# Image 0's queries and keys in a two-level form, and layer 1's value-output product ahead of them

## The chip, the cores and the metric

One core of a Trainium2 chip runs the whole kernel. Its engines are TensorE (PE in the profile, its weight loads PEld), VectorE (DVE), ScalarE (ACT), GpSimd (POOL) and SyncE (SP), whose queue issues nearly all DMAs here. The metric is the device time of one execution in microseconds; shown is the median of several runs.

## The reference

Two attention blocks, one after the other, on 8 images of 512 channels and 1024 positions, all in float32. Layer 0 has 8 heads of 64 channels; layer 1 has one head of 512.

```python
# layer 0
h = group_norm(x, gn_weight, gn_bias)              # 32 groups
qkv = einsum('oc,bct->bot', w_qkv, h) + b_qkv      # 8 heads: q, k, v of 64 channels
weight = softmax(einsum('bct,bcs->bts', q * scale, k * scale))
a = einsum('bts,bcs->bct', weight, v)
x = x + einsum('oc,bct->bot', w_proj, a) + b_proj
# layer 1
xn = group_norm(x, gamma, beta)                    # 8 groups
q, k, v = conv1x1(xn, q_w, q_b), conv1x1(xn, k_w, k_b), conv1x1(xn, v_w, v_b)
out = softmax(q^T k / sqrt(512)) v
x = x + conv1x1(out, p_w, p_b)
```

## The kernel before

**Products with fewer multiplications.** A convolution is a product of a 512x512 weight matrix with a 512x1024 image. The kernel makes it by the Strassen-Winograd scheme: both matrices are cut into 2x2 blocks, seven sums of blocks of each ("factors", 1 to 7) are multiplied pairwise, and sums of the seven products give the result. `wino` (L229) does this once: seven products, each of four matrix multiplications of 128x128 weights with 512 columns, so 28. `by_channel`, `by_token`, `biased` and `conv` are built on it. `conv2` (L536) with `inner_steps` (L452) does it twice: each of the seven products is again cut in halves, so there are 49 products of 128x128 weights with 256 columns. For that it needs the image's factors of factors (`inner_factors`, L423: seven times four subtractions of 128x256) and the weights' second sums (`keep2_steps`, L302: four operations of 128x896 on a weight tile, the results stored in DRAM by seven DMAs of 448 KB). `load_weight` brings them back from DRAM in the order of the list `uses`.

**Steps.** Within a convolution the products are taken in the order 1, 6, 2, 5, 7, then 3 and 4. The last two wait in the list `tail` and run after step 1 of what follows; `finish()` empties the list at once. In `inner_steps` step 1 fills a PSUM bank of pool "a", ScalarE copies it to a bank of pool "b" (L482), and step 6 adds onto this copy. `conv2` takes its seven outer products in the pairs (1, 5), (2, 6), (3, 4) and the single (7), the last two interleaved. `hooks` are functions that run behind each of these four parts, `background` a list from which each step takes one or more.

**The start** (`prologue`, L936). It loads the raw weights of layer 1, transposes keys and queries with `natural` (L893), multiplies them (`product`, "m": layer 1's scores need only this product of the two), normalizes image 0, and makes its values (`by_token`), queries and keys (`conv`, one level) with weights whose first sums `prepare` (L281) has made. Between these, the second sums of v are made on VectorE, those of q, k, m and p on GpSimd, for the later images. After the keys come the transposes of layer 1's value weights (wv), the bias rows (`bias_products`, L919) and the product "z" of layer 1's value and output weights. Then `attention0` of image 0 begins; z's own sums are made during it.

**Order.** A scheduler orders the instructions of each engine ahead of time; `tc.keep_in_program_order` pins one behind the one traced before it on its engine, and all TensorE work is pinned. Each engine, and each DMA queue, then works strictly in this order.

**Memory.** `big` is a pool of `NBIG` = 34 tiles of 4 KB a partition: images, factors, q, k, v, exponents and the results of sums on VectorE. `wpool` has 3 tiles for weights (14 KB a partition each). A tile's slot comes free when its last reader is done. PSUM has the pools "a", "b", "c" with two banks each, and "acc" with two.

Of the kernel before, what the change touches and what calls it, by code (L numbers as in the profile page):

```python
# [9 lines left out]
F32 = mybir.dt.float32  # L10
I32 = mybir.dt.int32
AF = mybir.ActivationFunctionType
# [3 lines left out]
P = 128  # L16
EPS = 1e-5
ORDER = (1, 5, 2, 6, 7, 3, 4)
NBIG = 34

# [9 lines left out]
def two_attention_blocks_kernel(  # L30
# [143 lines left out]
    def main_path(ctx):  # L174
# [46 lines left out]


        tail = []

# [76 lines left out]

        def keep2_steps(n, t, engine=nc.gpsimd, pin=lambda ins: ins):  # L302

            if engine is nc.gpsimd:
                u = wpool.tile([P, 4, 7, P], F32, tag="w", name=f"prepare2_{n}")
                u = [u[:, i, :, :] for i in range(4)]
            else:
                u = [big_tile(f"prepare2_{n}_{i}", (P, 7, P)) for i in range(4)]
            quarter = lambda k, i: t[:, :, k, ts(i, P)]
            a11, a21, a12, a22 = quarter(0, 0), quarter(0, 1), quarter(1, 0), quarter(1, 1)  # L310
            s1, s2, s3, s4 = u
            def store():
                for j, f in enumerate((a11, a12, s4, a22, s1, s2, s3)):
                    pin(nc.sync.dma_start(wdram2[n][:, :, j, :], f))

            return [
                *(
                    lambda dst=dst, x=x, y=y, op=op: tc.keep_in_program_order(engine.tensor_tensor(dst, x, y, op))
                    for dst, x, y, op in (
                        (s1, a21, a22, ALU.add), (s2, s1, a11, ALU.subtract), (s3, a11, a21, ALU.subtract),  # L320
                        (s4, a12, s2, ALU.subtract),
                    )
                ),
                store,
            ]

        def keep2(n, t, engine=nc.gpsimd):
            for f in keep2_steps(n, t, engine):
                f()
# [72 lines left out]

        def biased(out, bias):
            def done(i, r, c, ps, u):
                oc = 2 * r + i
                dst = out[oc][:, ts(c, HT)]
                if u is None:
                    nc.scalar.activation(dst, ps, AF.Identity, bias=bias[:, oc : oc + 1])
                else:
                    nc.vector.scalar_tensor_tensor(dst, ps, bias[:, oc : oc + 1], u, ALU.add, ALU.add)  # L410

            return done

        def channel_tiles(name):
            return [big_tile(f"{name}_{c}") for c in range(KC)]

        def conv(wf, hf, bias, name, **kw):
            out = channel_tiles(name)
            by_channel(wf, hf, name, biased(out, bias), **kw)
            return out  # L420


# [112 lines left out]

        def conv2(n, f, bias, name, hooks=(), after=(), by_tokens=False, alone=False):  # L536

# [42 lines left out]
            def pair(s, products, y, x, final, **kw):  # L580
# [5 lines left out]

                w = weights2[s // 2][:, (0, 2, 0, 1)[s] :]

                def mm(ps, j, start):
                    for i, p in enumerate(products):  # L590
                        wt = w[:, i, j - 1, :]
                        if not by_tokens:
                            matmul(ps[:, i, :], wt, f[p][j], start=start and i == 0, stop=True, skip_group_check=True)
                            continue
                        for h in range(2):
                            matmul(
                                ps[:, i, ts(h, P)], f[p][j][:, ts(h, P)], wt,
                                start=start and (i, h) == (0, 0), stop=True, skip_group_check=True,
                            )
# [13 lines left out]
            second = []  # L613
            weights2 = [weight_part((n, 0))]
            pair(0, (1, 5), [(1, 0), (1, 1)], None, [])[1]()
            pair(
                1, (2, 6), [(0, 0), (0, 1)], [(1, 0), (1, 0)], [load_weight, lambda: biased_half(0, 0)], defer=second,
            )[1]()
            weights2.append(weight_part((n, 1)))
            ahead, end = pair(  # L620
                3, (3, 4), [(0, 1), (1, 0)], [(0, 1), (1, 0)], [load_weight, *after],
                order=(-3, 6, 5, -4, 7, 2) if alone else (-3, 6, -4, 2, 5, 7),
# [296 lines left out]
        def bias_products(lhs):  # L919

            n = len(lhs)
            ps = acc_tile("ps_bias")
            for kc in range(KC):
# [12 lines left out]
        def prologue():  # L936
            ident.append(big_tile("ident", (P, P)))
            make_identity(nc, ident[0])
            raw_k = raw("k", 5)
            raw_q = raw("q", 4)  # L940
            h0 = [load_x(0, c, "h0") for c in range(KC)]
            first = {n: prepare(n) for n in "vqk"}
            wk = natural(raw_k, "k", ("a", "b"))
# [13 lines left out]
            )  # L957
            raw_v = raw("v", 6)
            raw_p = raw("p", 7)
            for f in first["v"][1]:  # L960
                f()
            background.extend(steps)
            background.extend(first["q"][1])
            v = by_token(weight_factors(first["v"][0]), hf, "v0_0", middle=(2, 5, 6, 7), back=4)
            finish()
            run_background(len(background))
            keep2("v", first["v"][0], nc.vector)
            background.extend(first["k"][1])
            x1 = [load_x(1, c, "x1") for c in range(KC)] if B > 1 else []
            norm1 = GroupNorm(0, "0_1")  # L970
            background.extend(lambda c=c: norm1.stats(c, x1[c]) for c in range(len(x1)))
            q = conv(weight_factors(first["q"][0]), hf, pcols("bq0"), "q0_0")
            keep2("q", first["q"][0])
            keep2("k", first["k"][0])
            t, steps = prepare("m")
            k = conv(weight_factors(first["k"][0]), hf, pcols("bk0"), "k0_0", hooks=[[], [], [], [], steps])
            finish()
            p0, p0_steps = prepare("p")
            raw_p0 = raw("p0", 3)
            keep2("m", t)  # L980
            wv = natural(raw_v, "v", "bc")
            norm1.group_mean(acc_tile("gmean_0_1")[:, :KC])
            for f in p0_steps:
                f()
            keep2("p", p0)
            keep("p", p0)
            bias = bias_products([(wk, "bq1"), (raw_p, "bv1"), (raw_p0, "bv0")])
            product(wv, raw_p, "z", bank="b")
            norm1.affine(acc_tile("gvar_0_1")[:, :KC])
            t, steps = prepare("z")  # L990
            load = lambda: load_weight(tc.keep_in_program_order)
            second = keep2_steps("z", t, pin=tc.keep_in_program_order)
            later = {
# [14 lines left out]
        def load_again(b, c, what):  # L1008
            t = big_tile(f"{what}_{b}_{c}")
            nc.sync.dma_start(t, spills[b][c])  # L1010
            return t

        def all_background():
            run_background(len(background))

# [456 lines left out]
```

## Time and profile before

| What | Value |
|---|---|
| Median of 3 runs | 2768.27 us (2767.59 to 2768.7) |
| The profiled execution | 2768.3 us |
| Its span, first to last instruction | 2765.8 us |
| Mean granted TensorE clock | 0.999 |
| Busy in 49.7 to 97.8 us (48.1 us): TensorE, VectorE, ScalarE, GpSimd | 48.10, 32.58, 5.09, 18.01 us |
| Busy in 97.8 to 117.9 us (20.1 us): the same | 19.58, 11.38, 2.90, 16.49 us |
| DMA in these two stretches | 0.82 and 0.63 of the 16 engines |

The first of these stretches holds image 0's queries and keys, the second the transposes of wv, the bias rows and z. In the lines of the profile `psa_q` is a bank of pool "a" in the queries' convolution, `ps_wz` one of the product z, `sc` a bank of scores, `av` one of values by attention. An fp32 multiplication shows as two entries. A line in the timeline gives start, length, engine, line of the kernel, operation, the tile written and those read, the count, and in brackets the idle time before it and what ended it.

### The profile page before, as it was taken

Reading aid. Unit: us, or ns where it says so; the run is one execution under the profiler, and the core shown is the slowest. Engines: PE = TensorE matmul, PEld = TensorE weight load, DVE = VectorE, ACT = ScalarE, POOL = GpSimd, SP = SyncE. Lnnn points to the kernel's source line nnn. Section 1 sums busy time; section 2 is a strip of 40 time slices with the busy share of each in tenths; the row PEclk is TensorE's granted clock in tenths of the full one; section 3 lists DMA queues with packets and bytes.
Section 4 is the critical chain, followed back from the end, with each engine's and each line's share of the span. In section 5 each row is a group of like instructions: output and inputs, shape, how many; then the busy total and the mean of one; then the engine's idle time right before and its main releaser. Section 6 shows DMA issues by size and latency. Waiting matters only on the chain.

```text
span 2765.8 us, 36809 instructions
## 1 busy us (share of the span) xinstructions
PE 2753.6 (100%) x13436; PEld 1762.1 (64%) x13436; DVE 2045.6 (74%) x3214; ACT 998.4 (36%) x1307; POOL 1291.4 (47%) x1384
## 2 busy tenths in 40 slices
PE   9999999999999999999999999999999999999999
PEld 5437736776376853868538694486844968348585
DVE  6587777777777777777777867777678776787776
ACT  1253454214632146312453125531255313633130
POOL 2313605745067440774307752176621766146763
PEclk9999999999999999999999999999999999999999
DMA  7827412344113441144401443114521145112302
GB/s 265 253 91 252 181 32 70 138 159 166 40 63 138 170 162 32 63 161 167 150 24 63 177 182 119 32 55 184 196 98 49 58 153 216 59 54 97 142 24 74
DMA packets 126070, 332.60 MB, mean 120 GB/s; under 512 B 19831, under 2 KB 64695, under 8 KB 114362
## 3 DMA queue, kind: packets, MB, share of 16 engines
q1 hardware_dynamic: 125294, 329.75, 33.6%
q8 instruction: 108, 1.77, 0.3%
q14 instruction: 80, 0.66, 0.1%
q10 hardware_dynamic: 588, 0.42, 0.1%
HBM read 258.14 MB, written 71.99 MB: 119 GB/s over the span
## 4 chain that ended last, share of the span: by engine, by line
PE 99%; DVE 1%; DMA 0%; issue 0%; SPq 0%; DVEq 0%
PE sc L60 16%; PE av L60 16%; PE psb_av L60 6%; PE psb L60 5%; PE psa_av L60 4%; PE psc_av L60 4%; PE psc L60 4%; PE psa L60 3%; PE psb_v L60 3%; PE psb_k L60 3%; PE psb_p L60 3%; PE psb_q L60 3%; PE psb_g L60 3%; PE psb_z L60 3%; PE psc_z L60 2%; PE psa_k L60 2%
## 5 line engine op out<-in xcount | busy, mean ns | idle before, releaser
L700 DVE TENSOR_TENSOR sum<-sum,e 128x1024 f32<-128x1024 f32 x384 | 473.9, 1234 | 35.5 <-ACT e L696 0.9
L696 ACT ACTIVATE e<-sc 128x1024 f32<-128x1024 f32 x512 | 476.1, 1053 | 63.1 <-PE sc L60 62.6
L60 PE MATMUL sc<-q,k 64*128 64x512 f32 x2048 | 456.8, 596 | 0.0
L60 PE MATMUL av<-e,v 128*64 128x512 f32 x2048 | 453.4, 595 | 0.0
L60 PEld LDWEIGHTS sc<-q,k 64*128 64x128 f32 x2048 | 190.1, 185 | 245.9 <-ACT e L696 120.9
L60 PEld LDWEIGHTS av<-e,v 128*64 128x64 f32 x2048 | 141.4, 137 | 299.0 <-issue 288.2
L434 POOL TENSOR_TENSOR inner_h<-x 128x256 f32<-128x256 f32 x16 | 14.8, 924 | 415.9 <-DVE x L1028 415.9
L698 DVE TENSOR_TENSOR sum<-e,e 128x1024 f32<-128x1024 f32 x64 | 79.9, 1249 | 103.6 <-ACT e L696 103.6
L719 ACT COPY a<-av 128x512 f32<-128x512 f32 x64 | 37.5, 586 | 320.1 <-PE av L60 280.6
L126 POOL TENSOR_TENSOR rstd<-ve,mhalf 128x4 f32<-128x4 f32 x16 | 18.8, 1177 | 274.0 <-DVE ve L124 274.0
L60 PE MATMUL psb<-inner,inner_h 128*128 128x256 f32 x448 | 115.6, 380 | 0.0
L60 PE MATMUL psa_av<-e,z 128*128 128x512 f32 x256 | 112.5, 592 | 0.0
L482 ACT COPY psb_v<-psa_v 128x512 f32<-128x512 f32 (+1 forms) x28 | 14.5, 517 | 232.5 <-DVE x L845 176.6
L60 PEld LDWEIGHTS psb<-inner,inner_h 128*128 128x128 f32 x448 | 84.5, 190 | 13.6 <-POOL inner L449 2.1
L60 PE MATMUL psb_z<-w_z,inner_h 128*128 128x128 f32 x672 | 87.5, 276 | 0.0
L60 PE MATMUL psb_g<-inner_h,w_m 128*128 128x256 f32 x336 | 84.9, 381 | 0.0
L776 ACT ACTIVATE e<-e 128x1024 f32<-128x1024 f32 x64 | 65.1, 1052 | 46.7 <-DVE e L766 25.6
L60 PEld LDWEIGHTS psb_z<-w_z,inner_h 128*128 128x128 f32 x672 | 81.4, 192 | 0.5
L60 PEld LDWEIGHTS psa_av<-e,z 128*128 128x128 f32 x256 | 47.4, 190 | 53.6 <-issue 51.7
L771 POOL TENSOR_TENSOR e<-e,e 128x512 f32<-128x512 f32 x64 | 79.3, 1271 | 2.0 <-DVE e L766 1.8
L571 POOL TENSOR_TENSOR v<-v,v 128x256 f32<-128x256 f32 x28 | 20.1, 726 | 125.3 <-DVE u_v L566 121.3
L820 POOL TENSOR_TENSOR t<-e,t 128x1024 f32<-128x1024 f32 x32 | 78.4, 2482 | 0.0
(443 smaller groups left out, 6138.0 us busy)
## 6 DMA issues: line engine op xcount, KB each, us to landing
r<-all_rows SPq DMA_DIRECT2D x78, 256.0 KB
x<-in_x SPq DMA_DIRECT2D x36, 512.0 KB
h<-in_x SPq DMA_DIRECT2D x32, 512.0 KB
spill<-x SPq DMA_DIRECT2D x32, 512.0 KB
x<-spill SPq DMA_DIRECT2D x32, 512.0 KB
out<-x SPq DMA_DIRECT2D x63, 256.0 KB
kept<-a SPq DMA_DIRECT2D x28, 512.0 KB
again<-kept SPq DMA_DIRECT2D x28, 512.0 KB
```

The source lines that it names most:

```text
L60: tc.keep_in_program_order(nc.tensor.matmul(*args, **kw))
L126: nc.gpsimd.tensor_tensor(rstd, ve, mhalf, ALU.pow)
L434: pin(engine.tensor_tensor(dst, x, y, ALU.subtract))
L482: nc.scalar.copy(ps["b"], ps["a"])
L571: nc.gpsimd.tensor_tensor(d, x, y, ALU.add)
L696: nc.scalar.activation(e, sc, AF.Exp, scale=(C // 8) ** -0.5)
L698: nc.vector.tensor_add(total, es[0], e)
L700: nc.vector.tensor_add(total, total, e)
L719: nc.scalar.copy(dst, av)
L771: nc.gpsimd.tensor_tensor(blocks(dst, r, cc)[0], blocks(x, r, cc)[0], blocks(y, r, cc)[0], ALU.add)
L776: nc.scalar.activation(e[c, cc, r], e[c, cc, r], AF.Exp, scale=scale)
L820: on = lambda *a: lambda: tc.keep_in_program_order(nc.gpsimd.tensor_tensor(*a))
```

## The change

- `NBIG` becomes 35. The identity matrix for the transposes leaves the big pool for the slot of the tile `line`.
- `keep2_steps` becomes `second_sums`. It also returns a function that gives factor j of outer factor p from the tiles in SBUF. With `inside` (the default) the third sum overwrites one quarter of the weight tile and the other three go to big tiles; without it a tile of the weight pool takes all four.
- `conv2` takes `own`: that function, in place of weights loaded from DRAM; it then calls no `load_weight`.
- In the prologue, the inner factors of image 0 are made on GpSimd behind the values' background work; wv's transposes, the bias rows and the product z come directly after the values. The second sums of q are made on VectorE, those of v and then of k on GpSimd.
- Image 0's queries and keys are made with `conv2` from these sums. Into their hooks go the second sums of k and m, the loads of m and p, and the group norm of image 1. p's sums and stores come after the keys.
- `bias_products` uses a bank of pool "c" where it used "acc"; wv's transposes use "a" and "acc" where they used "b" and "c". The raw weights of v, p0 and p are loaded ahead of k's four blocks. `biased` and `conv` go.

```diff
-NBIG = 34
+NBIG = 35
...
-        def keep2_steps(n, t, engine=nc.gpsimd, pin=lambda ins: ins):
-
-            if engine is nc.gpsimd:
-                u = wpool.tile([P, 4, 7, P], F32, tag="w", name=f"prepare2_{n}")
-                u = [u[:, i, :, :] for i in range(4)]
-            else:
-                u = [big_tile(f"prepare2_{n}_{i}", (P, 7, P)) for i in range(4)]
+        def second_sums(n, t, engine, pin=lambda ins: ins, inside=True):
+
             quarter = lambda k, i: t[:, :, k, ts(i, P)]
             a11, a21, a12, a22 = quarter(0, 0), quarter(0, 1), quarter(1, 0), quarter(1, 1)
-            s1, s2, s3, s4 = u
+            if inside:
+                s3 = a21
+                s1, s2, s4 = (big_tile(f"prepare2_{n}_{i}", (P, 7, P)) for i in range(3))
+            else:
+                u = wpool.tile([P, 4, 7, P], F32, tag="w", name=f"prepare2_{n}")
+                s1, s2, s3, s4 = (u[:, i, :, :] for i in range(4))
+            f2 = (a11, a12, s4, a22, s1, s2, s3)
+
             def store():
-                for j, f in enumerate((a11, a12, s4, a22, s1, s2, s3)):
+                for j, f in enumerate(f2):
                     pin(nc.sync.dma_start(wdram2[n][:, :, j, :], f))
 
-            return [
+            return lambda p, j: f2[j - 1][:, ORDER.index(p), :], [
...
-                w = weights2[s // 2][:, (0, 2, 0, 1)[s] :]
+                def weight_of(i, j):
+                    if own:
+                        return own(products[i], j)
+                    return weights2[s // 2][:, (0, 2, 0, 1)[s] + i, j - 1, :]
...
-            first = {n: prepare(n) for n in "vqk"}
+            first = {n: prepare(n) for n in "vq"}
+            raw_v, raw_p0, raw_p = raw("v", 6), raw("p0", 3), raw("p", 7)
+            first["k"] = prepare("k")
...
-            background.extend(steps)
-            background.extend(first["q"][1])
+            inner, ih = inner_factors(hf, "h0_0", tc.keep_in_program_order)
+            background.extend([*steps, *first["q"][1], ih[6], *ih[:6]])
             v = by_token(weight_factors(first["v"][0]), hf, "v0_0", middle=(2, 5, 6, 7), back=4)
             finish()
-            run_background(len(background))
-            keep2("v", first["v"][0], nc.vector)
...
-            q = conv(weight_factors(first["q"][0]), hf, pcols("bq0"), "q0_0")
-            keep2("q", first["q"][0])
-            keep2("k", first["k"][0])
-            t, steps = prepare("m")
-            k = conv(weight_factors(first["k"][0]), hf, pcols("bk0"), "k0_0", hooks=[[], [], [], [], steps])
+            all_background()
+
+            wv = natural(raw_v, "v", ("a", "acc"))
+            wq2, q_sums = second_sums("q", first["q"][0], nc.vector)
+            for f in q_sums[:4]:
+                f()
+            bias = bias_products([(wk, "bq1"), (raw_p, "bv1"), (raw_p0, "bv0")])
+            norm1, x1, made = GroupNorm(0, "0_1"), [load_x(1, c, "x1") for c in range(KC)], {}
+            for f in (q_sums[4], *second_sums("v", first["v"][0], nc.gpsimd)[1], *first["k"][1]):
+                f()
+            product(wv, raw_p, "z", bank="b")
...
+            wk2, k_sums = second_sums("k", first["k"][0], nc.gpsimd)
+            q = conv2(
+                "q", inner, pcols("bq0"), "q0_0",
+                [k_sums[:2], [lambda: ready("m")], k_sums[2:], [all_background]], own=wq2,
+            )
+            m_sums = second_sums("m", made["m"][0], nc.gpsimd)[1]
+            k = conv2(
+                "k", inner, pcols("bk0"), "k0_0",
+                [
+                    [lambda: norm1.group_mean(acc_tile("gmean_0_1")[:, :KC]), lambda: sum_up("m"), *m_sums[:2]],
+                    [lambda: norm1.affine(acc_tile("gvar_0_1")[:, :KC]), lambda: ready("p")], m_sums[2:], [],
+                ],
+                own=wk2,
+            )
             finish()
+            sum_up("p")
+            p0 = made["p"][0]
+            t, steps = prepare("z")
             keep2("p", p0)
             keep("p", p0)
```

`half_stats` of image 1 (eight of 128x512) go into `background` one by one, `ready(n)` calls `prepare(n)`, and `sum_up(n)` makes its first sums on VectorE.

## The prediction

> **What bounds the kernel now.** I read the page's first part, then the chain that ended last in order of time from 0 to 400 us, then the waits of TensorE, then the engines one by one from 25 to 175 us and from 232 to 302 us.
>
> ```profile
> span 2765.8 us, 36809 instructions
> ...
> PE 2753.6 (100%) x13436; PEld 1762.1 (64%) x13436; DVE 2045.6 (74%) x3214; ACT 998.4 (36%) x1307; POOL 1291.4 (47%) x1384
> ```
>
> TensorE (PE) is idle for 12.2 us of 2765.8. The table of its waits puts 3.8 us on the first weight load and 0.7 us on image 1's values; nothing in images 2 to 7. So only TensorE work that disappears, or a gap that closes, shortens the run; and any wait that TensorE gets lengthens it one for one. The change touches the stretch from 25 to 118 us. The chain there (start, length, what):
>
> ```profile
> 46.21 3.45 PE psc_v L60 x16
> 49.66 3.43 PE psa_q L60 x8
> ...
> 94.29 3.45 PE psc_k L60 x8
> 97.74 0.03 issue
> 97.77 0.76 DVE k L410
> 98.53 0.04 issue
> 98.57 1.64 PE tr_wv L63 x13
> 100.21 0.12 PE gmean L60 x2
> 100.33 3.54 PE ps_bias L60 x24
> 103.87 13.93 PE ps_wz L60 x32
> 117.80 0.12 PE gvar L60 x2
> 117.92 7.07 PE sc L60 x32
> ...
> 277.90 0.86 PE psa_q L60 x4
> ...
> 299.06 0.86 PE psa_p L60 x4
> ```
>
> Image 0's queries and keys take 49.66 to 97.74, 48.08 us, in 14 products of 3.43 us; then a wait for the keys' last eviction; then transposes, bias rows, the product z, and attention from 117.92. Image 1's queries, in the two-level form that the change brings to image 0, take 277.90 to 299.06, 21.16 us for the 49 products of 256 columns.
>
> **The two convolutions.** Removed: 48.08 us. Added: twice 21.16 = 42.32 us. Gain 5.76 us, all on the path.
>
> [...]
>
> **The moved product.** Transposes, bias rows, z and both group matmuls are issued as often as before, only ahead of the queries, or in the keys. In the waits of TensorE the transposes wait 0.52 us for the keys' eviction (three of the sixteen had run before). After the change they use the banks "a" and "acc", which the values left at 33 us, so this 0.52 us goes. The copies of the transposed weights (two of 0.65 us on VectorE (DVE), two of 0.54 on ScalarE (ACT)) stay hidden behind the bias rows (3.54 us).
>
> **A new wait at the queries' start.** Step 6 accumulates onto a bank that ScalarE copies from step 1's. Elsewhere the previous convolution's last two steps fill this time; after z nothing does, as the tail is empty.
>
> ```profile
> 278.80 0.57 ACT L482 COPY psb_q<-psa_q 128x512 f32<-128x512 f32 x1 [5.70 <-PE psa_q L60]
> ```
>
> In image 1 step 1's last entry is issued until 278.60 and the copy ends at 279.37: 0.77 us without cover. Bounds: 0, if z's last matmuls still drain under it, and 1.1 (before image 0's g the chain from last entry to next product took from 438.69 to 439.79). I take 0.77, by the nearest row. The keys' start is covered by the queries' tail (two products, 1.7 us).
>
> **Work beside it.** Now the engines that feed TensorE, on the new clock: values end 49.66, transposes 51.7, bias 55.2, z 69.2, queries 91.1, keys with 0.24 of group matmuls 112.5.
>
> GpSimd (POOL): 28 inner sums of 128x256 (image 1's L434 rows lie at 0.72 to 1.18 us, some 0.78 on average) are 22 us, from about 29, when the first t4 is there, to 51; the queries need them at 69. Then the values' second sums, four of 128x896:
>
> ```profile
> 54.66 9.87 POOL L318 TENSOR_TENSOR prepare_q<-prepare_q 128x896 f32<-128x896 f32 x4 [29.40 <-DMA sums_v<-prepare_v]
> 72.86 8.30 POOL L318 TENSOR_TENSOR prepare_k<-prepare_k 128x896 f32<-128x896 f32 x4 [8.34 <-DVE q L410]
> ```
>
> They took 8.3 us alone and 9.87 beside VectorE, so they end at about 61 to 64. The keys' first two follow, once VectorE has made the keys' first sums, by 75; the keys' last two are pinned behind the queries' third part (GpSimd adds of 0.73 us) at about 85 and end by 90. The keys need sum 2 at 93.7 (91.1 plus step 1 and the queries' tail, 2.6) and sum 3 at 96. Cover 6 us or more, so I cost them at nothing.
>
> VectorE: the weights' first sums, four of 128x512, show what GpSimd does to it when both inputs lie in SBUF:
>
> ```profile
> 58.13 4.46 DVE L292 TENSOR_TENSOR prepare_k<-prepare_k 128x512 f32<-128x512 f32 x2
> ...
> 93.55 1.89 DVE L292 TENSOR_TENSOR prepare_m<-prepare_m 128x512 f32<-128x512 f32 x3
> ```
>
> That is 0.65 us alone and 2.17 on average beside GpSimd, 1.5 more each. The queries' second sums (1.09 alone, L318 on VectorE at 50.31) become 1.09 to 2.6: from 53.1, after the copies, to 57.5 or 63.5; needed from 70.9 on. Then three bias copies (2.07), the keys' first sums (2.6), and image 1's statistics (eight of 0.64, four of 0.21: 6.0) beside the queries. The first addition that TensorE depends on comes at step 7, about 74.3, with 0.9 us of slack; VectorE has at most 63.5 + 2.1 + 2.6 = 68.2 behind it and some four statistics (3.0): 71.2. In time. During the queries it has the form's own 13.5 us (image 1's rows) plus the last statistics in 21 us. In the keys four m sums (2.6) stand ahead of the first part's tail; image 1 shows 2.4 us of VectorE idle there: 0 to 0.5 us late, I take 0.
>
> VectorE's lighter share before (per convolution four of 0.69 and six of 0.75, 7.3 us) makes room for nothing that TensorE waits on.
>
> DMA and the SP queue: raw v, p0 and p (12 issues of 256 KB, 0.67 us each as at 22.66 us) pass ahead of the keys' four loads, which start at some 23 instead of 15.4; their sums come at 66. The second sums go out in as many issues (seven of 448 KB each); q and v now leave before k, and m's four loads wait for v's slot (free at about 72), needed at 97. p's sums and stores slip into the first attention unit: p's second sums then share GpSimd with the exponent sums on VectorE, as z's did from 146.89 to 157.19, where no TensorE wait stands. Image 1's loads follow p's last store on SP, at about 130, for ScalarE at 135: before, ScalarE waited 0.68 us for them at no cost. Nothing.
>
> Slots: 35 big ones. At 60 us I count 18 for image 0's factors and values, 4 raw p and v, 3 sums of q, 3 of v, 4 of image 1, 1 bias row, up to 2 of z: 35. It just fits; a tile later and GpSimd or ScalarE waits for a store. The attention's start needs only the first head pair's keys, whose last part is added 0.9 us after its product, and the first scores read the half that was ready before: nothing, at most 1 us.
>
> **Sum**, against this execution's own 2768.3 us (2.5 of it around the span; the median of the runs is 2768.27): -5.76 - 0.52 + 0.77 = -5.51, so 2762.8 us. Bounds: best, the copy hidden and image 1's values' waits (0.7) gone as a slot more is free: 2761.3; worst without a mechanism of its own, 0.3 more of copy, 0.5 in the keys, 1 at the attention: 2764.6. A measurement of this kernel can tell about 0.2%, that is 5.5 us: the bound is 2762.7, inside this case.
>
> **Rivals.**
>
> B, VectorE late in the queries: its sums contend for all their length. For it: the 2.17 us rows, and a slack of only 0.9 us. If the keys' first sums also fall beside GpSimd (four of 2.17, 6 us more), the first addition comes 3 to 6 us late: 2766 (2764.6 to 2769). Against: GpSimd is done with the values by then.
>
> C, slower: GpSimd's queue stands still for a big slot. If the values' second sums find none of 35 free, the keys' sums stand behind them in the same queue, and slots come when q's own sums die at the queries' end, 91.1. Then six sums (2.08 to 2.47 us) stand ahead of the keys' step 6, with 2.6 us of cover: a wait of 9.9 to 12.2, so 2772.7 to 2775.0; at the contended price 2775. It decides from the point at which sum 2 is ready after 93.7; it makes the kernel slower once it is more than 5.5 us late, by over 0.2% from 11 us. For it: before, m's sums did wait 16.7 us for a slot that the keys' last product freed. Against: my count fits, and raw p and v free four at 69.2.
>
> D, it doesn't do what it says: the two-level form is no faster here, because its weights now come straight from sums in SBUF that are strided in other steps. If the 190 ns weight loads showed, twice in each of 98 products, TensorE would lose up to 37 us; from 0.3 of them on the gain of 5.5 and 5.5 more are gone: 2774 and up. Against: in images 1 to 7 the same shapes are loaded from SBUF and hide.
>
> **Chances.** My case 0.66 (own range 2761.3 to 2764.6; 0.44 below the bound of 2762.7, as its likeliest costs are nothing, 0.22 above it), B 0.17, all within 0.2%, C 0.12 and D 0.05, both slower by more. Faster 0.44, within 0.2% 0.39, slower 0.17. Range 2761 to 2770: it takes in B; outside it lie C and most of D, and some 0.04 below.
>
> **What would show it.** Right: query and key products in groups of 0.86, each convolution 21.2 us, z before them, attention at about 112.4; an idle of 0.8 us between step 1 and step 6 of the queries. B: TensorE waiting for an L566 addition between 74 and 80. C: a gap before the keys' step 6, released by GpSimd's second sums. Wrong altogether if waits appear in images 1 to 7, where I change nothing, or if the attention's first units wait for exponent sums.

## The result and the profile after

The changed kernel takes **2772.35 us**, the median of 22 runs (2769.11 to 2775.01); the kernel before, on the same chips, 2768.06 (22 runs, 2767.49 to 2768.94). The ratio is 1.0015 [1.0009, 1.0021]: 4.3 us slower, less than the 0.2% named above, but outside the forecast range of 2761 to 2770. The profiled execution took 2772.21 us, with this span and busy time (first part of its page):

```profile
span 2770.4 us, 37116 instructions
...
PE 2752.6 (99%) x13520; PEld 1779.5 (64%) x13520; DVE 2064.2 (75%) x3254; ACT 1007.2 (36%) x1323; POOL 1329.2 (48%) x1428
```

TensorE was idle for 12.2 us of its span before, and is now for 17.8. What was waited for (us in total, times, longest) answers to the waits named in the prediction:

```profile
PE psb_k L60 <- ACT psb_k L470: 3.1, 1, 3.1
PE sc L60 <- DVE k L552: 1.2, 2, 0.9
PE psb_q L60 <- issue: 0.8, 1, 0.8
PE psb_q L60 <- DVE q L554: 0.6, 1, 0.6
PE psc_v L60 <- DVE x L838: 0.5, 1, 0.5
```

The third line was in the prediction's sum; its own case had the others at nothing. The chain of waits where before it had values, queries, keys and then z (start, length, what):

```profile
46.08 3.45 PE psc_v L60 x16
49.53 1.75 PE tr_wv L63 x16
51.28 3.54 PE ps_bias L60 x24
54.81 13.95 PE ps_wz L60 x32
...
95.02 0.59 ACT psb_k L470
95.60 0.14 issue
95.74 1.10 PE psb_k L60 x4
```

**The keys' start.** Here the three engines are read side by side from 86 to 99 us. GpSimd (start, length, instruction; in brackets the idle time before and what ended it):

```profile
86.69 1.41 POOL L559 TENSOR_TENSOR q<-q 128x256 f32<-128x256 f32 x2
88.06 2.09 POOL L323 TENSOR_TENSOR prepare_k<-prepare_k 128x896 f32<-128x896 f32 x1
90.10 2.09 POOL L323 TENSOR_TENSOR prepare_k<-prepare_k,prepare_k 128x896 f32<-128x896 f32 x1
92.14 0.73 POOL L559 TENSOR_TENSOR q<-q 128x256 f32<-128x256 f32 x1
92.82 0.73 POOL L559 TENSOR_TENSOR q<-q,q 128x256 f32<-128x256 f32 x1
93.63 0.72 POOL L559 TENSOR_TENSOR q<-q 128x256 f32<-128x256 f32 x1
```

ScalarE:

```profile
92.90 0.72 ACT L566 ACTIVATE q<-q,par 128x512 f32<-128x512 f32 x1 [7.45 <-POOL q L559]
94.39 0.72 ACT L566 ACTIVATE q<-q,par 128x512 f32<-128x512 f32 x1 [0.76 <-POOL q L559]
95.02 0.58 ACT L470 COPY psb_k<-psa_k 128x512 f32<-128x512 f32 x1
```

TensorE:

```profile
91.59 1.03 PE L60 MATMUL psb_q<-inner_h,prepare_q 128*128 128x256 f32 x4
95.74 1.10 PE L60 MATMUL psb_k<-inner_h,prepare_k 128*128 128x256 f32 x4 [3.12 <-ACT psb_k L470]
...
98.12 1.91 PE L60 MATMUL psc_k<-inner_h,prepare_k 128*128 128x256 f32 x4
```

The keys' last two second sums (L323) stand in the middle of the queries' additions (L559), 4.1 us long. The bias of that half (L566) waits for the additions, and the keys' bank copy (L470) stands behind the bias in ScalarE's order. The copy that step 6 needs came at 95.02, though what it copies was there at some 90.7. And afterwards four entries take 1.71 us to the next start instead of 0.86 (from 98.12; their length is 1.91 instead of 1.03): the granted clock fell, as the table by stretches shows (busy us by engine, then PEclk, DMA share, GB/s):

```profile
92.00:95.00 3.00, 0.61 (x3) 0.19 (x1) 1.72 (x4) 1.33 (x2) 2.28 (x4) 1.00 1.07 321
95.00:98.00 3.00, 2.26 (x8) 1.99 (x9) 0.00 (x0) 1.18 (x3) 0.00 (x0) 0.82 0.99 299
98.00:101.00 3.00, 3.00 (x11) 2.38 (x10) 0.00 (x0) 1.17 (x2) 0.00 (x0) 0.61 0.27 91
```

(1 - 0.82) x 3 + (1 - 0.61) x 3 is 1.7 us of full clock lost, or half speed for 3.4 us: taken by 1 us, PEclk is 0.97 from 96, 0.50 from 97 to 100, 0.83 from 100 and 1.00 from 101 on. That is this execution's loss. In e2 below, which is the same program up to this point, the same wait of 3.12 us was followed by half speed for 6.8 us (PEclk 0.56, 0.50 and 0.80 in the three stretches of 3 us from 95 us on). So the loss differs between executions, and some of the 5.9 us between the fastest and the slowest run may come from it.

**The keys' end.** The same pattern: m's last two sums stand on GpSimd ahead of the keys' last three additions, VectorE and ScalarE wait for these, and the first scores for VectorE.

```profile
115.38 2.09 POOL L323 TENSOR_TENSOR prepare_m<-prepare_m 128x896 f32<-128x896 f32 x1
117.42 2.08 POOL L323 TENSOR_TENSOR prepare_m<-prepare_m,prepare_m 128x896 f32<-128x896 f32 x1
119.46 0.73 POOL L559 TENSOR_TENSOR k<-k 128x256 f32<-128x256 f32 x1
```

```profile
118.85 1.13 PE L60 MATMUL sc<-q,k 64*128 64x512 f32 x4
120.85 1.13 PE L60 MATMUL sc<-q,k 64*128 64x512 f32 x4 [0.87 <-DVE k L552]
122.35 3.09 PE L60 MATMUL sc<-q,k 64*128 64x512 f32 x12 [0.36 <-DVE k L552]
```

The first eight score tiles, 32 products, took 9.26 us; before, 7.07.

### The profile page after: what moved, and what is told of

Its sections match the earlier page's. It is cut to its first block, busy times and chain, and to the rows that moved or that the text cites. A ratio compares the mean times of both kernels' runs of the same rounds, so it can differ in the third digit from the quotient of the medians.

```text
span 2770.4 us, 37116 instructions
## 1 busy us (share of the span) xinstructions
PE 2752.6 (99%) x13520; PEld 1779.5 (64%) x13520; DVE 2064.2 (75%) x3254; ACT 1007.2 (36%) x1323; POOL 1329.2 (48%) x1428
## 3 DMA queue, kind: packets, MB, share of 16 engines
q1 hardware_dynamic: 125294, 329.75, 33.6%
q8 instruction: 109, 1.79, 0.3%
## 4 chain that ended last, share of the span: by engine, by line
PE 96%; DVE 2%; POOL 1%; DMA 1%; issue 0%; SPq 0%; ACT 0%; DVEq 0%; POOLq 0%
PE sc L60 16%; PE av L60 16%; PE psb_av L60 5%; PE psb L60 5%; PE psa_av L60 4%; PE psc_av L60 4%; PE psc L60 4%; PE psa L60 3%; PE psb_p L60 3%; PE psb_g L60 3%; PE psb_z L60 3%; PE psb_v L60 3%; PE psb_q L60 2%; PE psb_k L60 2%; PE psc_z L60 2%; PE psc_v L60 2%
## 5 line engine op out<-in xcount | busy, mean ns | idle before, releaser
L693 DVE TENSOR_TENSOR sum<-sum,e 128x1024 f32<-128x1024 f32 x384 | 481.2, 1253 | 35.9 <-DVE sum L693 1.4
L689 ACT ACTIVATE e<-sc 128x1024 f32<-128x1024 f32 x512 | 476.2, 1050 | 62.1 <-PE sc L60 61.4
L470 ACT COPY psb_v<-psa_v 128x512 f32<-128x512 f32 (+1 forms) x28 | 14.5, 517 | 232.5 <-DVE x L838 176.5
L60 PEld LDWEIGHTS psb<-inner,inner_h 128*128 128x128 f32 x448 | 84.5, 190 | 13.6 <-POOL inner L437 2.1
L559 POOL TENSOR_TENSOR v<-v,v 128x256 f32<-128x256 f32 x28 | 20.0, 726 | 126.2 <-DVE u_v L554 122.1
L470 ACT COPY psb<-psa 128x512 f32<-128x512 f32 x56 | 32.0, 571 | 128.3 <-PE psa L60 128.3
```

What stands on the lines that cost most here:

```text
L60: tc.keep_in_program_order(nc.tensor.matmul(*args, **kw))
L470: nc.scalar.copy(ps["b"], ps["a"])
L559: nc.gpsimd.tensor_tensor(d, x, y, ALU.add)
L689: nc.scalar.activation(e, sc, AF.Exp, scale=(C // 8) ** -0.5)
L693: nc.vector.tensor_add(total, total, e)
```

## The experiments

Times are medians, with the range of the runs; "ahead" and "behind" compare a stage's start in the profile with that of the kernel before (first scores there at 117.85).

**The queue at the keys' start: e1, e4, e5.**

```diff
e1: -[k_sums[:2], [lambda: ready("m")], k_sums[2:], [all_background]]
    +[k_sums[:2], [lambda: ready("m"), *k_sums[2:]], [], [all_background]]
```

> Theory Q (a queue behind GpSimd): in the changed kernel TensorE's 3.1 us wait at the keys' start comes from three GpSimd additions of the queries' third part that stand behind the keys' sums 3 and 4 (2 x 2.09 us); ScalarE's bias operation on that half waits for them, and the keys' bank copy stands behind it. With sums 3 and 4 ahead of the queries' additions, the wait falls under 0.5 us, the half-speed stretch of TensorE that follows it (1.7 us) goes too, and the time falls by 4 to 5 us, to about 2767.8. Rival X (the clock drops by itself there): the wait goes, the half-speed stretch stays: 2769.3. Rival N (the later images lose on their own): the keys gain 4.8 but it is lost again by the end: above 2770.5.

2768.11 us (2766.34 to 2769.61), ratio 0.9999 [0.999, 1.0008]. The wait and the half-speed stretch are gone, 4.2 us under the changed kernel. GpSimd now does the queries' additions in one go, and step 6 follows the queries' tail directly:

```profile
92.45 1.03 PE L60 MATMUL psb_k<-inner_h,prepare_k 128*128 128x256 f32 x4
```

> Leaves out the queries' bias on the second half of positions for channels 256 to 511 (the two ScalarE operations that wait for GpSimd); all sums stay where the changed kernel has them. Theory Q: ScalarE's queue is free, so the keys' bank copy runs at once and TensorE's 3.1 us wait goes with its slow stretch, although GpSimd's order is unchanged; at most a smaller wait for the keys' sum 3 or a bank of pool c is left. About 2768.5 (2767.5 to 2770). Rival D (the keys wait for their own second sums, which end at 92.2): the wait stays at 2.5 us or more: 2772.

```diff
e4: -2, (7,), [(1, 0)], [(0, 1)], [lambda: biased_half(1, 1)], flush=second,
    +2, (7,), [(1, 0)], [(0, 1)], [lambda: name == "q0_0" or biased_half(1, 1)], flush=second,
```

2767.11 us (2766.03 to 2768.16), in a kernel that leaves out this part of the queries' bias: with GpSimd's order as it was, the wait is gone. So it was the queue behind the bias, not the keys' lack of their own sums.

```diff
e5: +def fill_up():
    +    ps = acc_tile("fill")
    +    for _ in range(6):
    +        matmul(ps[:, : 2 * P], gm[:, 0, :], inner[1][1], start=True, stop=True)
```

> The changed kernel, with six extra products of 256 columns (into a bank that nothing reads) put between the queries' tail and the keys' step 6; GpSimd's and ScalarE's orders as they are. It separates the wait itself from the clock. Theory: the keys' bank copy still ends at the same time, so TensorE still loses 3.1 us at the keys' start, but it is busy for 2.6 us of them, the granted clock stays at 1.0 through the keys, and the 1.7 us lost to one half-speed stretch of 3.4 us come back: about 2770.6 us, with a narrower spread than the 5.9 us of the changed kernel's runs. Rival: the half-speed stretch has nothing to do with the idle time; it stays, and the time stays at 2772.3.

2771.78 us (2770.96 to 2774.04). Step 6 starts at 95.84, as late as before, but the clock is 1.00 in every stretch, and the first scores start 1.6 us earlier than in the changed kernel, as expected. Both kernels then lose the same 2.2 us within the first scores; after these e5 alone waits 0.7 us for an exponent sum, and 0.8 us of the gain are left when image 1 starts. The idle time did cost the clock in the profile; half of what came back was spent again at the next wait. The medians differ by 0.6 us, which is within the noise.

**The first scores: e2, e3, e6, e10, e16.**

```diff
e2: -[... ready("p")], m_sums[2:], [],
    +[... ready("p")], [], [],
     finish()
    +for f in m_sums[2:]: f()
e3: e1 and e2
```

> Theory Q: the same happens at the keys' end, where m's sums 3 and 4 stand ahead of the keys' last three additions; the first scores, whose bank the keys' last additions on VectorE must leave, lose 2.2 us. With m's two sums behind the convolution, attention's first eight score tiles take 7.1 us without a wait; the keys' start is as before. Time lower by 2 us, to about 2770.3. Rival (the attention waits for the keys' values themselves, which come late with the two-level form however GpSimd's queue is ordered): 1 us or less is gained.

> Both moves. Theory Q: the gains add up, 6 to 7 us, to about 2765.5, so 2.5 us faster than the kernel before; what then still parts it from my forecast of 2762.8 is VectorE's wait for image 1 in the queries (0.6 us) and some 1 to 1.5 us in images 1 to 3. Rival (GpSimd's work only moves on: p's second sums and VectorE's exponent sums get later): less than 5 us gained, with waits in the first attention units.

e2: 2774.75 us (2772.8 to 2777.28), 2.4 slower than the changed kernel; e3: 2769.84 (2767.91 to 2770.85), 1.7 slower than e1. Of e2's 2.4 us some 1.3 are the longer half-speed stretch at the keys' start, which its edit doesn't touch; in e3 there is none, and image 1 starts 1.2 us later than in e1. The scores no longer wait, but m's and p's sums on GpSimd now both fall beside VectorE's exponent sums, and TensorE waits 3.4 us for these (two waits, 1.8 the longest). e3's rival held: the work only moved on.

```diff
e6: e1, and conv2 takes early=, run between the tail and step 6 of pair 0:
    +early=[lambda: sum_up("m"), *m_sums]
e10: e6, with z's last quarter put in the tail behind the queries' step 1, and
    +early=[lambda: norm1.group_mean(...), lambda: sum_up("m"), *m_sums]
e16: e10, with sum_up("m") in the queries' last hook
```

> The keys' last two second sums one hook earlier (as in e1), and now the weights m's first and second sums directly behind the queries' tail, ahead of all of the keys' parts, so that GpSimd has them done some 8 us before the keys' third part's additions. Theory: the first scores no longer wait (1.9 us of waits for VectorE's last keys' additions in the changed kernel), and unlike in e2 and e3 nothing is pushed into the first attention, so its 3.4 us of waits do not appear: the first scores start some 4 us earlier than in the kernel before and are still about 4 us ahead after attention's first unit. With the 2.4 us that e1 lost in images 1 to 4: about 2766 us. Rival: GpSimd's four sums slow VectorE in the keys' first two parts by as much (they take VectorE's additions from 0.76 to 1.5 or more), and the time stays at e1's 2768.

2771.22 us (2768.13 to 2773.28), 5 us more than expected. The first scores no longer wait, and no wait for exponent sums comes in, but the keys' second part waits. VectorE of e6:

```profile
96.08 1.88 DVE L115 TENSOR_TENSOR d<-mv,gmean 128x4 f32<-128x4 f32 x1
97.99 0.16 DVE L117 TENSOR_TENSOR d<-d 128x4 f32<-128x4 f32 x1
98.19 1.92 DVE L119 TENSOR_TENSOR dv<-d,mv 128x4 f32<-128x4 f32 x1
100.03 0.68 DVE L554 TENSOR_TENSOR k<-psc_k,u_k 128x512 f32<-128x512 f32 x1
```

and GpSimd and TensorE of e6 beside it:

```profile
95.86 2.08 POOL L323 TENSOR_TENSOR prepare_m<-prepare_m 128x896 f32<-128x896 f32 x1 [5.93 <-PE gmean L60]
98.02 2.07 POOL L323 TENSOR_TENSOR prepare_m<-prepare_m,prepare_m 128x896 f32<-128x896 f32 x1
```

```profile
101.36 3.78 PE L60 MATMUL psb_k<-inner_h,prepare_k 128*128 128x256 f32 x8 [3.68 <-DVE k L554]
```

Two additions of four numbers per partition lasted nearly as long as GpSimd's sum of 896, and ended with it; the one between two sums took 0.16. Behind TensorE's 3.7 us idle the clock fell again (PEclk 0.84, 0.50 and 0.53 in three stretches of 3 us from 98 us on). That is 3.4 us of full clock, of which 0.7 fell into the idle time itself, so it cost another 2.7.

> e7 with image 1's group mean (two products, four VectorE operations on 128x4) ahead of the weights m's sums instead of behind them. In e6 and e7 two of these small operations took 1.88 and 1.92 us beside GpSimd's sums, where 0.16 is their time alone, and TensorE waited 3.7 us for the keys' first addition behind them, then ran one stretch of 6.8 us at half clock (3.4 lost). Theory: both go, 7.0 us less at the first scores than e7, so these start 5 us ahead of the kernel before; nothing is lost in the first attention, 1.2 us in images 1 to 4: about 2765. Rival: VectorE's additions of the keys, which read one factor in SBUF, are slowed by GpSimd too, and the wait stays at 2 us or more: 2768 or more.

2767.68 us (2765.99 to 2768.66): the small operations take 0.16 again, the wait is 1.4 us and the clock stays at 1.00. It is 2.7 over the expectation: the keys' first two additions still stood behind the m sums on VectorE, and in swapped order, so that VectorE sat idle for 1.2 us ahead of them; and from image 1 on 2.6 were lost.

> e10 with the weights m's four first sums on VectorE moved from behind the queries' last additions to ahead of them, where VectorE is idle for 0.85 us; GpSimd's m sums start as early as these allow. In e10 TensorE waits 1.44 us at 98 us for the keys' first two additions on VectorE, which stand behind the m sums and in swapped order. Theory: the additions come in their order at some 96.3 to 97.7, the wait goes, the first scores start 1.4 us earlier than in e10 (3.7 ahead of the kernel before): 2766.3. Rival: the queries' last additions, now 1.8 us later, hold banks that the keys need, and the wait only moves: 2767.7.

**2765.34 us** (2764.06 to 2766.41), ratio to the kernel before 0.9989 [0.998, 0.9998]. The wait is 0.5 us (one of the small operations stands beside GpSimd's sums again, 1.93 us long), the first scores start 3.5 us ahead, and no time is lost in the first attention.

**The queries' start: e7, e11, e17.** e7 is e6 with z's last quarter in the tail, as in e10.

> e6 with the last quarter of the product z (four products, 3.4 us) issued behind the queries' first step instead of ahead of it, so that ScalarE's copy of the first bank is covered. Theory: the 0.75 us wait at the queries' start goes: 0.7 us under e6, about 2765.3. Rival: the copy of z's third quarter is late for the bank and the wait only changes its name: e6's time.

2771.88 us (2769.33 to 2772.66), 0.7 more than e6, which is within the noise. ScalarE's copy is covered, the wait of 0.75 is gone, and one of 1.1 us for VectorE stands in its place, some 5 us later (0.6 in the changed kernel): there a statistic waits 1.16 us for image 1's last load, and the first addition is behind it. The rival's time held, but not its cause, the copy of z's third quarter.

> e10 with image 1's statistics placed from the queries' second part on, in between VectorE's additions, instead of all ahead of them. Theory: VectorE's first addition of the queries no longer stands behind a statistic that waits 1.2 us for image 1's load, TensorE's wait of 1.1 us at 76 us goes, and the statistics, one per step of 0.64 us, fit between the additions: 1 us under e10, about 2764. Rival: the statistics now push additions that TensorE needs, and what is gained at 76 us comes back as several waits of 0.3 us in the queries: e10's time.

2769.95 us (2767.97 to 2771.96): all eight statistics between the additions cost two waits of 2.2 and 0.8 us, worse than what they replaced.

> e16 with the statistics of image 1's last quarter alone placed behind VectorE's first two additions of the queries, where VectorE is idle for 1.5 us; the other three quarters stay. Theory: TensorE's wait of 1.1 us at 73 us goes and nothing comes in its place (e11, which moved all four quarters in between, got 2.2 and 0.8 us of other waits): 1.0 us under e16, 2764.3. Rival: the last quarter's two statistics delay the next additions as e11's did: e16's 2765.3.

```diff
e17: e16, and
    -background.extend(... half_stats(c, i) for c in range(KC) ...)
    +background.extend(... half_stats(c, i) for c in range(KC - 1) ...)
    +last_stats, in the queries' hook 0: the last quarter's two, in program order
```

**2764.36 us** (2763.68 to 2765.48), ratio 0.9987 [0.9978, 0.9996]. Both waits of the queries are gone, the first scores start 5.2 us ahead, and this is still so when image 1 ends. It is 3.7 us under the kernel before and 8.0 under the changed one.

**The other half of the change alone: e8.** The kernel before, with the transposes, bias rows and z moved as in the change, and image 1's two group products in the keys. The two-level form without the move wasn't run.

> The kernel before with the transposes, bias rows and product z moved ahead of the queries as the change has them (raw weights loaded earlier, banks a, acc and c), but queries and keys still in one level, 14 products of 512 columns each two entries. It does the other half of the change alone. Theory: only the transposes' wait of 0.52 us for the keys' last eviction goes, and no wait comes in at the queries' start since the one-level form needs no bank copy; the first scores then wait for the keys' last eviction (some 0.8 us) as the transposes did: 2767.5 to 2768.5, no change. Rival: the move itself costs something later (image 1's loads and statistics, slots), and it is 1 us or more slower, which would put part of the changed kernel's loss on the move and not on the two-level form.

2781.84 us (2780.43 to 2782.8), 13.6 slower, against an expectation of no change. The first scores start 0.7 us ahead. But z's 13.9 us had been most of what m's and p's sums ran under: before, GpSimd made them from 97.86 to 117.19, while TensorE was at the transposes, the bias rows and z. Now they run beside the exponent sums. VectorE and TensorE of e8:

```profile
128.65 14.66 DVE L700 TENSOR_TENSOR sum<-sum,e 128x1024 f32<-128x1024 f32 x6
```

```profile
152.48 1.08 PE L60 MATMUL sums<-sum,ones 128*32 128x256 f32 x8 [6.49 <-DVE sum L700]
```

Six exponent sums take 14.66 us there, and 7.87 in the kernel before. TensorE waits 6.5 and 2.3 us for such sums, and the clock is at half speed for some 10.2 us, from within the first wait on. The moved product is costly by itself; the change avoids most of that cost by making m's sums in the keys.

**From image 1 on: e9, e12, e13, e14, e15, e18.** From image 1's values to TensorE's last product the changed kernel lost another 1.2 us, e1 2.4 and e10 2.6, in a program that is the same as before but for the 35 slots.

> The kernel before with 35 slots instead of 34, nothing else: the one part of the change that reaches images 2 to 7. In the changed kernel and in all its variants about 1 us goes lost in images 1 to 4, most of it where VectorE waits for a load of the next image in a values product (psc_v <- DVE x). Theory: the slots have no part in it, and that loss comes from the times at which the transfers meet; this kernel shows no such wait and stays at 2768.2. Rival: with 35 slots the loads of the next image get slots that are released later, the waits of psc_v for DVE x appear here too, and it is 0.8 to 1.5 us slower, 2769 to 2769.7.

2769.65 us (2768.8 to 2770.26). No such wait is there, and up to 2661 us, in image 7's last products, TensorE's stages start within 0.03 us of the kernel before: 35 slots by themselves don't bring the waits. The median is 1.5 us higher. In the profile 0.3 us come from a wait for ScalarE at 2661 us, and 1.8 lie after VectorE's last operation (6.6 us to the end of the span in place of 4.8); they weren't followed up.

> e11 with 34 slots, as the kernel before has. Theory: if the loss in images 1 to 4 hangs on which slots the next image's loads get, it changes here by up to 1 us either way, while the first scores start within 0.3 us of e11's. Rival: with one slot less the queries' and keys' sums or image 1's loads wait for a slot in image 0, and the first scores start 1 us or more later.

2771.18 us (2770.06 to 2772.67): the first scores start 0.4 us later than in e11, and 3.4 us are lost later, where e11 lost 1.7. Neither forecast fits: with 34 slots this program loses more than the 1 us that the theory allowed, and why stays open. What else meets there? In the changed kernel VectorE waits for the third load of a next image, and TensorE for VectorE:

```profile
912.66 0.69 DVE L91 BATCH_NORM_STATS2 bnst<-ahead 128x6 f32<-128x512 f32 x1 [0.77 <-DMA ahead<-in_x]
```

That load is issued at 907.31. The DMA queues from 907.3 to 907.8 (packets, MB, share of 16 engines):

```profile
q1 hardware_dynamic: 31, 0.06, 28.8%
q14 instruction: 1, 0.01, 8.6%
```

The one packet of kind `instruction`, by its name a piece of an engine's program and called a program fetch here, is counted on the same 16 engines as the data: 8.6% beside 28.8%. Likewise at 350 us, where VectorE stops for 0.47 us between two exponent sums, and about 1 us later, between 351.0 and 351.5, another such packet stands (q14, 0.01 MB, 3.8%):

```profile
350.25 3.88 DVE L693 TENSOR_TENSOR sum<-sum,e 128x1024 f32<-128x1024 f32 x3 [0.47 <-DVE sum L693]
```

If these fetches make the waits, the waits must move with the number of instructions ahead of them. So instructions that do nothing were put in before the first data arrive:

```diff
e13: e10 +for _ in range(15): matmul(pad[0:32, 0:32], ones, ones, ...)   (twice)
e14: e10 +for _ in range(20): nc.vector.memset(pad, 0.0)
e15: e10 and both;  e18: e17 and both
```

> e10 with 30 products of 32x32 (read by nothing) on TensorE while it waits for the first weights; all later program blocks of TensorE begin 30 instructions earlier. In e10 VectorE waits twice for the third load of a next image (1.00 us at 907 and 0.95 us at 1581 us), and TensorE 0.78 and 0.73 behind it; a load of TensorE's program (16 KB, queue q8) falls at 1578, inside the second late load, and a smaller one (8 KB, q14) at 902, inside the first. Theory: a program load on the same transfer engines makes the data late; with TensorE's blocks some 8 us earlier the second wait goes and the first stays: 0.7 us under e10, 2767.0. Rival: the late loads have another cause, both waits stay: 2767.7.

> e10 with 20 writes of 128x4 (read by nothing) on VectorE before the first data arrive, so that VectorE's program blocks begin 20 instructions (some 15 us) earlier. Theory: the 8 KB load at 902 us is VectorE's, and so is the one at 341.7 us beside its stop of 0.47 us between two exponent sums; both move, the wait at 907 goes (0.8 us for TensorE), the stop of 0.47 us moves to another place where it may or may not cost something; the wait at 1581 stays: 2766.6 to 2767.2. Rival: it is another engine's program or another cause, and the waits stay where they are: 2767.7.

> e10 with both of these paddings. Theory: both waits go, 1.5 us under e10: about 2766.2. Rival: 2767.7 as e10.

> e17 with both paddings of e15. Theory: the late load at 1578 us in e16 (0.99 us, 0.8 us for TensorE) follows the programs' blocks and is gone or at another image; by the program loads alone one can't say whether another one comes in, so 0.8 us less to 0.3 us more than e17. Rival: it stays at 1578.

VectorE's waits for a load of the next image, us, by the image's place (about 905, 1241 and 1579 us):

| kernel | 905 | 1241 | 1579 | VectorE's stops of 0.46 to 0.47 at | median us (range) |
|---|---|---|---|---|---|
| before | 0 | 0 | 0 | 168 | 2768.06 (2767.49 to 2768.94) |
| e10 | 1.00 | 0 | 0.95 | 212, 342, 742, 2460 | 2767.68 (2765.99 to 2768.66) |
| e13, TensorE's program shifted | 0.92 | 0.62 | 0 | 211, 342, 742, 2459 | 2767.32 (2766.2 to 2768.38) |
| e14, VectorE's shifted | 0 | 0 | 0.99 | 2445 | 2766.97 (2765.62 to 2768.22) |
| e15, both | 0 | 0.76 | 0 | 2445 | 2767.54 (2766.5 to 2768.4) |
| e17 | 0.82 | 0 | 0.78 | none | 2764.36 (2763.68 to 2765.48) |
| e18, both | 0 | 2.01 | 0 | none | 2764.24 (2763.42 to 2766.08) |

The first late load and the stops follow VectorE's program, the others TensorE's. Over twelve profiles (before, the changed kernel, e1, e9, e10, e12 to e18) there are 60 places from image 3 on at which the third and fourth load of a next image are issued together; of the 17 with a program fetch from 2 us before to 1.5 after their issue, VectorE waited in 15; of the other 43 in none. (Over all twenty profiles: in 27 of 31, and in none of 69.) In the medians e13 to e15 and e18 can't be told from the kernels they were made from: a wait avoided in one image came back in another. That the late loads go with the fetches, and move with them, is shown in the profiles; what they cost over many runs isn't. (The profiled execution of e18 took 2765.59 us.)

## Why the prediction was wrong

The sum was -5.76 - 0.52 + 0.77. **All three terms held.** The products run in groups of 0.86 us, as in image 1 before (21.16 / 49 = 0.432 us for one of 256 columns, against 3.43 / 4 = 0.858 for 512); the transposes start at 49.53, directly behind the values; the queries' first wait is 0.75. So rival D is out; its 190 ns is the mean of a weight load in image 0's and image 1's queries before, and the changed kernel's queries have the same 190. The inner sums took from 28.75 to 50.86, 22 us; v's second sums ended at 62.1, q's at 63.1, inside what was given; for q's that was partly luck, as each took 2.2 to 3.0 us where 1.09 to 2.6 was given, but they began 0.9 us earlier. The sum failed in what was **costed at nothing**. In the profiled execution, span against span:

| step, as the prediction put it | given | measured, us |
|---|---|---|
| "Cover 6 us or more, so I cost them at nothing" (the keys' last two sums) | 0 | 3.12, and 1.7 of clock behind it |
| "nothing, at most 1 us" (the attention's start) | 0 | 2.2 |
| VectorE's first addition, "In time" | 0 | 0.60 |
| "images 1 to 7, where I change nothing" | 0 | 1.2 |
| not listed: rest up to the first scores, pieces of up to 0.3 each | 0 | 1.1 |
| not listed: from the first values by attention to image 1 | 0 | 0.2 |

That is 10.1 us; -5.5 and 10.1 make the 4.6 by which the span grew. The rest up to the first scores is what the other rows leave; most of it stands where TensorE starts again behind a wait.

**The step that failed** is the first. Its times were nearly right: "at about 85 and end by 90"; the sums ran from 88.06 to 92.19, ahead of the 96 at which the keys would need the first of them, sum 3. But the question was only when the sums are needed. What stands behind them in GpSimd's queue wasn't asked, though the hook that issues them runs inside the queries' third part: three additions, the bias on ScalarE that waits for these, and the bank copy that ScalarE does in order. "The keys' start is covered by the queries' tail" spoke of TensorE alone and missed that the tail's own last additions share a queue with the copy. e1 and e4 remove the wait from either end of that queue. Rival C had the right place (the keys' step 6) and the right queue, with another mechanism: GpSimd never stood for a slot there. (It stood 8.83 us before the first of the keys' sums, until a DMA of the bias columns; sum 2 was ready at 75.2 all the same.)

**The attention's start** is the same error once more: "the first scores read the half that was ready before" holds for the half's products, not for its additions on GpSimd behind m's sums. **Rival B's** wait is there with another cause: not contention, the sums ended at 63.1, but a load of image 1 that VectorE's statistics waited for in front of the addition (1.57 us):

```profile
74.07 1.29 DVE L91 BATCH_NORM_STATS2 bnst<-x 128x6 f32<-128x512 f32 x2 [1.57 <-DMA x<-in_x]
```

"Nothing" for image 1's loads looked at those that ScalarE needs at 135. The four for VectorE's statistics, issued at 60.8 to 69.1 us in place of 55.5 to 59.2, weren't priced. **The clock** and **the program fetches** weren't in the working at all.

With the queries' start covered, the two gains of the sum are 5.76 + 0.52 = 6.3 us, and e17 has 5.2 of them at the first scores. So the gain was there; the order of the side work spent it.

## What to carry to other kernels

When side work is hooked into a queue, ask not only when its result is needed but what is issued behind it on that engine, and follow that to the next engine in order until TensorE: here two sums of 2.1 us held up three additions, a bias and a copy. A product that is moved takes its cover away from what ran under it (13.6 us slower in e8); list the side engines' work in its old place, too. Close TensorE's longest waits between products first: here those of 3.12 us (the changed kernel and e2) and 3.7 us (e6) cost 1.7, 3.4 and 2.7 us of clock on top.

## What the runs showed of the hardware

- **The clock.** An idle time of 3.12 us was followed by half speed for 3.4 us in the changed kernel and for some 6.8 us in e2, one of 3.7 us (e6) by some 6.8 us ((0.16 + 0.50 + 0.47) x 3 = 3.4 of full clock), one of 6.5 us (e8) by some 10.2 us, and ones of 1.4 us (e10), 2.2 us (e11) and 2.3 us (e8) by none; with the gap filled (e5) by none. The 3.9 us that TensorE stood until the first weights, in the changed kernel, were followed by none (PEclk 1.00 from 2 to 20 us). So the length of the gap alone doesn't set the loss; what else does wasn't shown.
- **VectorE beside GpSimd.** VectorE additions with both inputs in SBUF took longer beside GpSimd's sums: 1.88 us for 128x4 in e6 (0.16 alone), ending with GpSimd's sum, and 2.44 on average for an exponent sum (14.66 / 6 in e8; 7.87 / 6 = 1.31 in the kernel before, with GpSimd idle). An addition with one input in PSUM took no longer: 0.68 us for 128x512 (`u_q<-psb_q,t_q`, at 57.53 in the kernel before) beside GpSimd's sums for q, which run from 54.66 to 64.53, and 0.68 (`k<-psc_k,u_k`, at 103.19 in the changed kernel) with GpSimd idle.
- **Program fetches.** The packets of kind `instruction` hold some 16 KB on q8 (1.79 MB in 109) and 8 KB on q14 (0.66 MB in 80; both from the changed kernel's page), and take 0.3% and 0.1% of the 16 engines, where the data of q1 take 33.6%. VectorE's waits for loads beside them are 0.6 to 2.0 us and its stops 0.46 to 0.47, and both move when instructions are added far ahead (e13 to e15).
